# Latent attention: output products from seven half-block products, and half of the divisions moved to ScalarE

## Chip, core and metric

The kernel runs on one core of one Trainium2 chip. The metric is the device time of one execution in microseconds (us); the time before is 2025.44 us, the median of three runs (2025.08, 2025.44, 2031.71).

## The reference, cut to what matters

The program is a stack of eight layers on x, two sequences of 512 tokens with 512 features each, all in float32. The change touches the third and the fifth layer. The fifth is latent attention with 32 heads:

```python
x = x + L0_attn_a(layernorm(x)); x = x + L0_ffn(layernorm(x))
x = x + L0_attn_b(layernorm(x)); x = x + L0_ffn(layernorm(x))   # attn_b: grouped queries
x = x + L1_attn_a(layernorm(x)); x = x + L1_ffn(layernorm(x))   # attn_a: latent attention
...
def L1_attn_a(x, wq_a, q_norm_w, wq_b, wkv_a, kv_norm_w, wkv_b, wo):
    q = rms_norm(x @ wq_a.T, q_norm_w) @ wq_b.T          # 32 heads, 128 + 64 features
    kv_c, k_pe = split(x @ wkv_a.T)                      # 64 latents, 64 rotary features
    k_nope, v = split(rms_norm(kv_c, kv_norm_w) @ wkv_b.T)
    scores = (q_nope . k_nope + rope(q_pe) . rope(k_pe)) * scale, causal
    out = softmax(scores) @ v                            # (b, s, 32 * 128)
    return out @ wo.T                                    # wo.T: (4096, 512)
```

## The kernel before

`attn_mla` keeps the values as 64 latents per token. For every group of eight heads (`grp`, four of them) `fold_values` multiplies the value weights into the output weights, head by head, into one tile `fold` of 512 x 512 (four chunks of 128 partitions, two heads of 64 latents in each). The context of eight heads is then a tile `ctxT` of 512 latents x 512 tokens, and the output of the group is the product of the two, added to x.

The work goes over eight pairs `m` of a head group and a sequence (`grp`, `b`), with `b` changing fastest, and over eight heads `h` in each: 64 units. The first eight units are in `opening`; the other 56 are in the loop at L1594. Per unit the loop issues:

- on every even head, `queries` for the heads two further on (TensorE, 3 us) and `rotate`: two instructions on VectorE (L1461, L1462), and three on GpSimd (L1465 and twice L1468);
- `exponents`: four rows of score products (L274), and for each row one masked minimum on VectorE (L285) and one exponential on ScalarE (L295);
- `normalise`: a reciprocal on VectorE (L303), and the division of the four rows (128, 256, 384 and 512 wide) by four GpSimd instructions (L310);
- `turned_head`: two block transposes of the head before on VectorE (L322, L323).

Beside the heads of pair `m` the function `beside` finishes the pair before it. At `h` = 1 `values` runs the value products (L350) and copies the four banks to `ctxT` (L364, L365). At `h` = 3, 4, 6 and 7 `output` makes the product for one tile of 128 tokens by a chain of four matmuls of 128x128 by 512 (L183), and adds it to x on VectorE (L250). Where `b` is 1, `fold_values` runs at `h` = 0 and `fold_keys` at `h` = 4 and 5. After the last unit, `m` = 8 has the values and outputs of the last pair alone, with the layer norms of the first sequence for the next layer beside them.

TensorE and VectorE run in the order in which the code is written here (`manual_schedule`); ScalarE's and GpSimd's instructions in the loop are put in order by the framework's scheduler, by priority and readiness. All of PSUM is one tile `held` of eight banks, which `turn` hands out in a ring; `reserve` takes one bank out of the ring.

The third layer, `attn_gqa`, already makes its output products (L1163) as seven products of half blocks for all but its last pair: `out_sums` (L1115) and `context_sums` (L1130) form the sums of blocks on GpSimd (L1127, L1137 to L1140), `out_product` (L1145) makes a product and adds it to the rows with `add_quarter` (L247). Its divisions are all on ScalarE (L308).

Of the kernel before, what the change touches and what calls it, by code (L numbers as in the profile page):

```python
# [31 lines left out]
F32 = mybir.dt.float32  # L32
# [3 lines left out]
ALU = mybir.AluOpType  # L36
# [10 lines left out]
class Block:  # L47
# [251 lines left out]

    def normalise(self, probs, total, scalar=False):  # L300

        inv = self.sm(NT, "invs")
        self.nc.vector.reciprocal(inv, total)  # L303
        for qt in range(NT):
            row = probs[:, self.ROW[qt] : self.ROW[qt] + self.KEYS[qt][1] - self.KEYS[qt][0]]
            each = inv[:, qt : qt + 1]
            if scalar:
                self.nc.scalar.activation(row, row, AF.Identity, scale=each)  # L308
            else:
                self.nc.gpsimd.tensor_scalar(row, row, each, 1.0, ALU.mult, ALU.mult)  # L310
# [604 lines left out]


def attn_gqa(k, a, bound, block):

# [9 lines left out]
    with ExitStack() as ctx:  # L928
# [162 lines left out]
        def softmax(m, j):  # L1091
            probs = k.other().rearrange("p t s -> p (t s)")
            k.normalise(probs, k.exponents(qs.pop((m, j)), keys[m], probs), scalar=True)
            return probs
# [13 lines left out]

        left, right = slice(0, D // 2), slice(D // 2, D)
        sums = [lp.tile([P, 2, S // 2], F32, tag="c_sum", name="c_sum", bufs=3) for i in range(3)]  # L1110
        room = [k.w.tile([P, 3, D // 2], F32, tag="w3", name="wo_sum", bufs=6) for i in range(2)]
        held = [(0, 0), (0, 1), (0, 2), (1, 0), (1, 1), (1, 2)]
        outs = {}

        def out_sums(m, part):  # L1115

            wo = w[m]["wo"]
            b11, b12, b21, b22 = (  # L1120
                [wo[:, 2 * r + i, c] for i in range(2)] for r in range(2) for c in (left, right)
            )
            t1, t2, t4 = ([room[n][:, o] for n, o in held[2 * i : 2 * i + 2]] for i in range(3))
            steps = (t1, b12, b11), (t2, b22, t1), (b12, b22, b12), (t4, b21, t2)
            for out, x, y in steps[2 * part : 2 * part + 2]:
                for i in range(2):
                    nc.gpsimd.tensor_tensor(out[i], x[i], y[i], ALU.subtract)  # L1127
            outs[m] = b11, b21, b22, t1, t2, b12, t4

        def context_sums(m):  # L1130
            c = ctxs[m]
            a11, a12, a21, a22 = (
                c[:, 2 * r : 2 * r + 2, t] for t in (first, second) for r in range(2)
            )
            s1, s2, s4 = sums
            op = nc.gpsimd.tensor_tensor
            op(s1, a21, a22, ALU.add)  # L1137
            op(a21, a11, a21, ALU.subtract)
            op(s2, s1, a11, ALU.subtract)
            op(s4, a12, s2, ALU.subtract)  # L1140
            ctxs[m] = a11, a12, a22, s1, s2, a21, s4

        begun = {}

        def out_product(m, n):  # L1145


            a11, a12, a22, s1, s2, s3, s4 = ctxs[m]
            b11, b21, b22, t1, t2, t3, t4 = outs[m]
            lhsT, rhs = {  # L1150
                1: (a11, b11), 2: (a12, b21), 3: (s4, b22), 4: (a22, t4),
                5: (s1, t1), 6: (s2, t2), 7: (s3, t3),
            }[n]
            after = n in (5, 6)
            if n == 1:
                begun[m] = k.reserve()
            ps = begun[m] if n in (1, 5, 6) else k.turn()
            if n == 5:
                k.reserved = None
            for t in range(2):  # L1160
                out = ps[:, bass.ts(t, D // 2)]
                for i in range(2):
                    nc.tensor.matmul(  # L1163
                        out, lhsT[:, i, bass.ts(t, P)], rhs[i],
                        start=not (after or t or i), stop=i == 1, skip_group_check=True,
                    )
            at = groups[m][1] * NT
            for rows, columns in {
                1: ((0, left),), 2: ((0, left),), 3: ((0, right),), 4: ((2, left),),
                5: ((0, right), (2, right)), 6: ((2, left),), 7: ((2, left), (2, right)),  # L1170
            }[n]:
                k.add_quarter(at + rows, columns, ps)

# [12 lines left out]
        def beside(m, j):  # L1186
# [9 lines left out]
            if before is not None and j == 1:  # L1196
                values(before)
                if m < len(groups):
                    spread_values(m)
                if summed:  # L1200
                    context_sums(before)
            if m == G - 1 and j < 2:
# [18 lines left out]
            if summed and 0 < j < 3:  # L1221
                out_sums(before, j - 1)
            if before is not None and not summed and j > 1:
# [54 lines left out]
def attn_mla(k, a):  # L1278
# [9 lines left out]
    with ExitStack() as ctx:  # L1288
# [7 lines left out]
        def load(g):  # L1296
            w = dict(
                qn=k.load(a["m_wqn"][g], [P, J, QL], "w3", 6),
                wk=k.load(a["m_wk"][g], [P, J, KL], "w3", 6),
                wv=k.load(a["m_wv"][g], [P, J, KL], "w3", 6),  # L1300
                wo=k.load(a["m_wo"][g], [P, J, D], "w8", 5),
                lat=lp.tile([P, J, KL], F32, tag="q_lat", name="q_lat", bufs=3),
                pe=lp.tile([P, J, 64], F32, tag="q_pe", name="q_pe", bufs=3),
                rest=lp.tile([P, J, 64], F32, tag="q_rest", name="q_rest", bufs=3),
            )
            nc.sync.dma_start(out=w["pe"], in_=a["m_wpe0"][g])
            nc.sync.dma_start(out=w["rest"][64:128], in_=a["m_wpe1"][g])
# [283 lines left out]
        with tc.manual_schedule(engines=engines | {mybir.EngineType.Activation, mybir.EngineType.Pool}):  # L1591
            opening()
        with tc.manual_schedule(engines=engines):
            for n in range(E, len(units) + E):  # L1594
# [514 lines left out]
def _layout(i):  # L2109
# [60 lines left out]
    wkvb = i["L1_attn_a_wkv_b"].reshape(8, 4, 256, 64)  # L2170
    o["m_wk"] = wkvb[:, :, :128].transpose(0, 2, 1, 3)
    o["m_wv"] = wkvb[:, :, 128:].transpose(0, 2, 1, 3)
    o["m_wo"] = i["L1_attn_a_wo"].T.reshape(8, 4, P, D).transpose(0, 2, 1, 3)
# [38 lines left out]
```

## Time and profile before

| What | Value |
| --- | --- |
| median of three runs | 2025.44 us |
| the profiled execution: time, span from first to last instruction | 2033.69 us, 2031.7 us |
| TensorE matmul (PE) busy | 1950.3 us, 96% |
| VectorE (DVE), ScalarE (ACT), GpSimd (POOL) busy | 68%, 43%, 51% |
| granted TensorE clock, mean over the span | 0.985 |
| `attn_gqa`, most of it (300 to 1110 us): PE busy | 801 of 810 us |
| `attn_mla`, the loop (1208 to 1598 us): PE busy | 374.47 of 390 us |
| in the loop: DVE, ACT, POOL busy | 254.12, 185.02, 222.74 us |

Times of single instructions are in ns, stretches and sums in us from the start of the span. A float32 matmul shows as two records, so that a chain of four matmuls is eight records. A record's duration is longer than the step from one record to the next, since matmuls are pipelined; what a product occupies on TensorE is read from start to start.

### The profile page before, as it was taken

Reading aid. Unit: us, or ns where it says so; the run is one execution under the profiler, and the core shown is the slowest. Engines: PE = TensorE matmul, PEld = TensorE weight load, DVE = VectorE, ACT = ScalarE, POOL = GpSimd, SP = SyncE. Lnnn points to the kernel's source line nnn. Section 1 sums busy time; section 2 is a strip of 40 time slices with the busy share of each in tenths; the row PEclk is TensorE's granted clock in tenths of the full one; section 3 lists DMA queues with packets and bytes.
Section 4 is the critical chain, followed back from the end, with each engine's and each line's share of the span. In section 5 each row is a group of like instructions: output and inputs, shape, how many; then the busy total and the mean of one; then the engine's idle time right before and its main releaser. Section 6 shows DMA issues by size and latency. Waiting matters only on the chain. (4 is left out here: it accounts for less than half of the span.)

```text
span 2031.7 us, 40110 instructions
## 1 busy us (share of the span) xinstructions
PE 1950.3 (96%) x15424; PEld 1171.7 (58%) x15424; DVE 1390.0 (68%) x3585; ACT 882.8 (43%) x2350; POOL 1036.5 (51%) x1212
## 2 busy tenths in 40 slices
PE   9889989999999999999999999999999899997999
PEld 5333346777777777777775544454544545654554
DVE  8778748767776677767775577666566675845854
ACT  3676723444444444444442365444545211631451
POOL 4411146687755678777752175555465634224221
PEclk9988999999999999999999999999999999998999
DMA  4010212122221223222222220020201003002001
GB/s 137 11 42 1 73 63 73 53 84 98 101 73 44 83 78 103 100 81 74 73 75 90 76 83 26 5 73 1 73 1 43 6 6 47 2 2 41 2 2 42
DMA packets 69789, 108.92 MB, mean 54 GB/s; under 512 B 13522, under 2 KB 50386, under 8 KB 62548
## 3 DMA queue, kind: packets, MB, share of 16 engines
q1 hardware_dynamic: 68660, 103.10, 16.2%
q8 instruction: 125, 2.05, 0.4%
q10 hardware_dynamic: 640, 1.05, 0.3%
q0 software_dynamic: 288, 2.10, 0.3%
q14 instruction: 76, 0.62, 0.1%
HBM read 80.00 MB, written 4.19 MB: 41 GB/s over the span
## 5 line engine op out<-in xcount | busy, mean ns | idle before, releaser
L295 ACT ACTIVATE room<-room,nmax 128x128 f32<-128x128 f32 (+3 forms) x384 | 212.9, 558 | 354.4 <-DVE nmax L285 351.5
L274 PE MATMUL held<-kT,q 128*32 128x64 f32 (+15 forms) x4096 | 264.1, 396 | 20.0 <-DVE invs L303 12.5
L285 DVE CUSTOM_DVE_ANT_0 room<-held,mask 128x128 f32<-128x128 f32 (+3 forms) x384 | 179.0, 487 | 82.7 <-PE held L274 76.9
L274 PEld LDWEIGHTS held<-kT,q 128*32 128x32 f32 x4096 | 141.5, 110 | 111.8 <-issue 30.3
L350 PE MATMUL held<-turned,vals 32*128 32x384 f32 (+7 forms) x2784 | 187.8, 416 | 1.3 <-issue 1.3
L587 DVE TENSOR_REDUCE nm<-held 128x1 f32<-128x512 f32 x256 | 161.8, 682 | 36.9 <-PE held L617 31.0
L350 PEld LDWEIGHTS held<-turned,vals 32*128 32x128 f32 (+1 forms) x2784 | 149.5, 167 | 37.8 <-issue 23.0
L308 ACT ACTIVATE room<-room,invs 128x128 f32<-128x128 f32 (+3 forms) x256 | 122.8, 550 | 31.3 <-DVE invs L303 31.2
L323 DVE STREAM_TRANSPOSE turned<-room 128x1152 f32<-128x1152 f32 x80 | 108.2, 1365 | 35.1 <-ACT room L308 21.6
L236 POOL TENSOR_TENSOR rstd<-ve,mhalf 128x1 f32<-128x1 f32 x64 | 37.8, 594 | 174.7 <-DVE ve L234 170.4
L183 PE MATMUL held<-fold,ctxT 128*128 128x512 f32 x256 | 117.8, 604 | 0.6 <-ACT ctxT L364 0.6
L247 DVE TENSOR_TENSOR rows<-rows,held 128x512 f32<-128x512 f32 x135 | 89.4, 681 | 36.3 <-PE held L1163 35.8
L1070 POOL TENSOR_TENSOR q<-q,room 128x256 f32<-128x256 f32 x64 | 45.4, 731 | 127.5 <-DVE q L1053 124.0
L295 ACT ACTIVATE probs<-probs,nmax 128x128 f32<-128x128 f32 (+3 forms) x128 | 71.1, 556 | 66.5 <-DVE nmax L285 65.3
L310 POOL TENSOR_SCALAR probs<-probs,invs 128x128 f32<-128x128 f32 (+3 forms) x128 | 66.0, 536 | 59.6 <-DVE invs L303 57.5
L1088 POOL TENSOR_TENSOR q<-q,cosq 128x512 f32<-128x512 f32 x60 | 85.9, 1432 | 20.5 <-DVE t L1085 20.5
L1044 PE MATMUL held<-room,w 128*128 128x256 f32 x384 | 95.1, 384 | 0.0
L183 PE MATMUL sc<-w,room 128*128 128x512 f32 x208 | 92.7, 592 | 0.0
L579 PEld LDWEIGHTS held<-keys,qs 32*128 32x128 f32 x256 | 31.1, 189 | 101.4 <-DVE nm L587 71.2
L1089 POOL TENSOR_TENSOR q<-q,t 128x512 f32<-128x512 f32 x64 | 86.3, 1348 | 5.6 <-DVE q L1088 1.9
L1465 POOL TENSOR_TENSOR t<-t,sinq 128x512 f32<-128x512 f32 x31 | 39.6, 1279 | 95.9 <-DVE invs L303 95.9
L1163 PE MATMUL held<-w,ctxT 128*128 128x256 f32 x360 | 86.5, 383 | 0.5 <-ACT ctxT L364 0.5
(349 smaller groups left out, 4982.3 us busy)
## 6 DMA issues: line engine op xcount, KB each, us to landing
w<-in_b_wq SPq DMA_DIRECT2D x16, 1024.0 KB, 4.8
w<-in_b_wo SPq DMA_DIRECT2D x16, 1024.0 KB, 5.0
vals<-v SPq DMA_DIRECT2D x256, 64.0 KB, 2.0
w<-in_m_wo SPq DMA_DIRECT2D x8, 1024.0 KB, 5.3
w<-in_b_wk SPq DMA_DIRECT2D x16, 256.0 KB, 2.7
w<-in_b_wupv SPq DMA_DIRECT2D x16, 256.0 KB, 2.6
w<-in_m_wqn SPq DMA_DIRECT2D x8, 384.0 KB, 3.0
rows<-in_x SPq DMA_DIRECT2D x8, 256.0 KB, 4.7
```

The lines of the kernel that those rows point to most:

```text
L183: last = self.nc.tensor.matmul(out, lhsT, rhs, start=(i == 0), stop=(i == len(pairs) - 1))
L247: self.nc.vector.tensor_tensor(x, x, ps.rearrange("p (t d) -> p t d", t=2), op)
L274: nc.tensor.matmul(ps[32 * i : 32 * i + 32, a - lo : b - lo], q[:, at : at + 32], keys[:, a:b], start=True, stop=True,)
L285: nc.vector.tensor_tensor_reduce(out=row, in0=ps[:, :kv], in1=self.mask_back[:, :kv] if qt % 2 else self.mask[:, S - kv :], op0=ALU.add, o ...
L295: nc.scalar.activation(row, row, AF.Exp, bias=nmax, scale=-1.0, accum_out=total[:, qt : qt + 1])
L308: self.nc.scalar.activation(row, row, AF.Identity, scale=each)
L323: self.nc.vector.transpose(out[:, :last], probs[:, :last])
L350: self.nc.tensor.matmul(out[:, :, :n], values(i, j), rhs, start=(j == blocks[0]), stop=(j == stop[i]),)
L587: k.latest = nc.vector.tensor_reduce(nm[u % 2][:, qt, at : at + 1], ps, AX.X, ALU.max, negate=True).ins
L1044: nc.tensor.matmul(out, lhsT[:, c], rhs[:, c], start=c == 0, stop=c == 1)
L1089: nc.gpsimd.tensor_tensor(q, q, t2, ALU.add)
L1163: nc.tensor.matmul(out, lhsT[:, i, bass.ts(t, P)], rhs[i], start=not (after or t or i), stop=i == 1, skip_group_check=True,)
```

## The change

In `attn_mla` the output of a pair is no longer four chains but seven products of half blocks. The context C (tokens x latents) and the folded weights M (latents x features) are cut into 2 x 2 blocks of 256 x 256. Each product is two tiles of 128 tokens by two chunks of 128 latents: four matmuls of 128x128 by 256. The sums of blocks that they need are formed on GpSimd: per pair four of the context (`context_sums`, in two parts at `h` = 2 and 3), per head group six instructions for the weights (`weight_sums`, in two parts at `h` = 1 and 2 of the pair with `b` = 1; one block of `fold` is overwritten). `STEPS` puts products 1 and 2 at `h` = 3, 6 and 4 at `h` = 4, 5 and 3 at `h` = 6, and 7 at `h` = 7; `TAIL` is the order for the last pair. Product 1's bank is reserved; 6 and 5 are accumulated on top of it, so that it is read three times and comes back to the ring after product 5. The seven products are added to x by nine additions of 128 x (2 x 256).

In the loop of `attn_mla` the rows of 128 and of 512 are divided on ScalarE, those of 256 and 384 on GpSimd as before; `opening` is unchanged in this. The key and value weights of four heads come in by one DMA in place of two. `attn_gqa` uses the same class now; there two of its sums of weight blocks are one instruction of 512 each in place of two of 256, and the second and third context sum change places.

```diff
-    def normalise(self, probs, total, scalar=False):
+    def normalise(self, probs, total, scalar=()):
...
-            if scalar:
+            if qt in scalar:
                 self.nc.scalar.activation(row, row, AF.Identity, scale=each)
             else:
                 self.nc.gpsimd.tensor_scalar(row, row, each, 1.0, ALU.mult, ALU.mult)
...
+class HalfBlocks:
+    LEFT, RIGHT = slice(0, D // 2), slice(D // 2, D)
+    ADDED = {
+        1: ((0, LEFT),), 2: ((0, LEFT),), 3: ((0, RIGHT),), 4: ((2, LEFT),),
+        5: ((0, RIGHT), (2, RIGHT)), 6: ((2, LEFT),), 7: ((2, LEFT), (2, RIGHT)),
+    }
...
+    def weight_sums(self, key, wo, part):
+        a, b = self.held
+        op = lambda out, x, y: self.k.nc.gpsimd.tensor_tensor(out, x, y, ALU.subtract)
...
+        t1, t4 = a[:, 0:2], b[:, 1:3]
+        t2 = a[:, 2], b[:, 0]
+        if part == 0:
+            op(t1, b12, b11)
+            for i in range(2):
+                op(t2[i], b22[:, i], t1[:, i])
+        else:
+            op(b12, b22, b12)
+            for i in range(2):
+                op(t4[:, i], b21[:, i], t2[i])
...
+    def context_sums(self, c, part=None):
...
+        if part != 1:
+            op(s1, a21, a22, ALU.add)
+            op(s2, s1, a11, ALU.subtract)
+        if part != 0:
+            op(a21, a11, a21, ALU.subtract)
+            op(s4, a12, s2, ALU.subtract)
+        self.context = {1: a11, 2: a12, 3: s4, 4: a22, 5: s1, 6: s2, 7: a21}
+
+    def product(self, key, n, at):
+        k = self.k
+        lhsT, rhs = self.context[n], self.of[key][n]
+        after = n in (5, 6)
+        if n == 1:
+            self.begun = k.reserve()
+        ps = self.begun if n == 1 or after else k.turn()
+        if n == 5:
+            k.reserved = None
+        for t in range(2):
+            out = ps[:, bass.ts(t, D // 2)]
+            for i in range(2):
+                k.nc.tensor.matmul(
+                    out, lhsT[:, i, bass.ts(t, P)], rhs[i],
+                    start=not (after or t or i), stop=i == 1, skip_group_check=True,
+                )
+        for rows, columns in self.ADDED[n]:
+            k.add_quarter(at + rows, columns, ps)
...
-                wk=k.load(a["m_wk"][g], [P, J, KL], "w3", 6),
-                wv=k.load(a["m_wv"][g], [P, J, KL], "w3", 6),
+                wkv=k.load(a["m_wkv"][g], [P, 2, J, KL], "w3", 6),
...
-        def output(grp, b, t):
-            ps = k.turn()
-            c = ctxs[grp, b]
-            k.chain(ps, [(c[:, i, bass.ts(t, P)], ms[grp][:, i]) for i in range(J)])
-            k.add_to_x(b * NT + t, ps)
+        def begin_sums():
+            room = k.w.tile([P, 3, 2, S // 2], F32, tag="w8", name="c_sums", bufs=5)
+            return HalfBlocks(k, [room[:, i] for i in range(3)])
...
+        STEPS = {3: (1, 2), 4: (6, 4), 6: (5, 3), 7: (7,)}
+        TAIL = {3: (1, 2), 4: (4, 6), 6: (3, 5), 7: (7,)}
...
+            if before and h in (1, 2) and before[1] == 0:
+                halves.weight_sums(before[0], ms[before[0]], h - 1)
+            if before and h in (2, 3):
+                halves.context_sums(ctxs[before], h - 2)
             if before and h in (3, 4, 6, 7):
-                output(*before, (3, 4, 6, 7).index(h))
+                for n in (TAIL if last else STEPS)[h]:
+                    halves.product(before[0], n, before[1] * NT)
...
                 if n < len(units):
-                    k.normalise(probs[n % 2], total)
+                    k.normalise(probs[n % 2], total, (0, NT - 1))
```

More of the change, by code (lines that the diff above doesn't have):

```diff
@@ L914, in ffn_lora, with __init__ @@
                 k.layernorm(t, k.turn, back=True)
+class HalfBlocks:
+    LEFT, RIGHT = slice(0, D // 2), slice(D // 2, D)
+    ADDED = {
+        1: ((0, LEFT),),
+        2: ((0, LEFT),),
+        3: ((0, RIGHT),),
+        4: ((2, LEFT),),
+        5: ((0, RIGHT), (2, RIGHT)),
+        6: ((2, LEFT),),
+        7: ((2, LEFT), (2, RIGHT)),
+    }
+    def __init__(self, k, sums):
+        self.k, self.sums, self.of = k, sums, {}
+        self.held = [
+            k.w.tile([P, 3, D // 2], F32, tag="w3", name="wo_sum", bufs=6) for i in range(2)
+        ]
+    def weight_sums(self, key, wo, part):
+        a, b = self.held
+        op = lambda out, x, y: self.k.nc.gpsimd.tensor_tensor(out, x, y, ALU.subtract)
+        b11, b12, b21, b22 = (
+            wo[:, 2 * r : 2 * r + 2, c] for r in range(2) for c in (self.LEFT, self.RIGHT)
+        )
[9 more added lines that the diff above has]
+                op(t4[:, i], b21[:, i], t2[i])
+        pair = lambda x: (x[:, 0], x[:, 1])
+        self.of[key] = {
+            1: pair(b11), 2: pair(b21), 3: pair(b22), 4: pair(t4), 5: pair(t1), 6: t2, 7: pair(b12)
+        }
+    def context_sums(self, c, part=None):
+        first, second = slice(0, S // 2), slice(S // 2, S)
+        a11, a12, a21, a22 = (c[:, 2 * r : 2 * r + 2, t] for t in (first, second) for r in range(2))
+        s1, s2, s4 = self.sums
+        op = self.k.nc.gpsimd.tensor_tensor
+        if part != 1:
[20 more added lines that the diff above has]
+                    start=not (after or t or i), stop=i == 1, skip_group_check=True,
+                )
+        for rows, columns in self.ADDED[n]:
+            k.add_quarter(at + rows, columns, ps)
@@ L1092, in softmax @@
             probs = k.other().rearrange("p t s -> p (t s)")
-            k.normalise(probs, k.exponents(qs.pop((m, j)), keys[m], probs), scalar=True)
+            k.normalise(probs, k.exponents(qs.pop((m, j)), keys[m], probs), range(NT))
             return probs
@@ L1107, in output @@
             k.add_to_x(groups[m][1] * NT + t, ps)
-        left, right = slice(0, D // 2), slice(D // 2, D)
         sums = [lp.tile([P, 2, S // 2], F32, tag="c_sum", name="c_sum", bufs=3) for i in range(3)]
[L1111 to L1143, printed above, removed]
@@ L1145, in out_product @@
-        def out_product(m, n):
[L1148 to L1172, printed above, removed]
+        halves = HalfBlocks(k, sums)
@@ L1174, in attn_gqa @@
+        def out_product(m, n):
+            halves.product(m, n, groups[m][1] * NT)
         units = [(m, j) for m in range(len(groups)) for j in range(J)]
@@ L1200, in beside @@
                 if summed:
-                    context_sums(before)
+                    halves.context_sums(ctxs[before])
             if m == G - 1 and j < 2:
@@ L1221, in beside @@
             if summed and 0 < j < 3:
-                out_sums(before, j - 1)
+                halves.weight_sums(before, w[before]["wo"], j - 1)
             if before is not None and not summed and j > 1:
@@ L1305, in load @@
             )
+            w["wk"], w["wv"] = w["wkv"][:, 0], w["wkv"][:, 1]
             nc.sync.dma_start(out=w["pe"], in_=a["m_wpe0"][g])
@@ L1592, in attn_mla @@
             opening()
+        halves = begin_sums()
         with tc.manual_schedule(engines=engines):
@@ L2170, in _layout @@
     wkvb = i["L1_attn_a_wkv_b"].reshape(8, 4, 256, 64)
-    o["m_wk"] = wkvb[:, :, :128].transpose(0, 2, 1, 3)
-    o["m_wv"] = wkvb[:, :, 128:].transpose(0, 2, 1, 3)
+    o["m_wkv"] = wkvb.reshape(8, 4, 2, 128, 64).transpose(0, 3, 2, 1, 4)
     o["m_wo"] = i["L1_attn_a_wo"].T.reshape(8, 4, P, D).transpose(0, 2, 1, 3)
```

## The prediction

> **What bounds the kernel now.** I read the page, then the busy times of stretches, since a share over eight layers says nothing of one of them.
>
> ```profile
> core 0: us, PE busy (x) PEld busy (x) DVE busy (x) ACT busy (x) POOL busy (x), PEclk, DMA share, GB/s
> 300.00:1110.00 810.00, 801.01 (x6778) 592.28 (x6779) 578.54 (x1245) 344.11 (x957) 543.65 (x539) 1.00 0.25 78
> 1208.00:1598.00 390.00, 374.47 (x4203) 196.61 (x4191) 254.12 (x745) 185.02 (x567) 222.74 (x311) 1.00 0.10 34
> ```
>
> The first row is most of `attn_gqa`, the second the loop of `attn_mla`. In both TensorE is all but full, at the full granted clock. In the loop VectorE has 136 us free of 390, ScalarE 205, GpSimd 167. Next, what TensorE waits for there, in the view of waits:
>
> ```profile
> PE held L274 <- DVE invs L303: 11.1, 11, 1.1
> PE held L350 <- issue: 1.9, 2, 1.3
> PE held L350 <- DVE room L323: 1.3, 1, 1.3
> PE held L274 <- POOL q L1468: 1.2, 1, 1.2
> PE held L183 <- ACT ctxT L364: 0.6, 1, 0.6
> ```
>
> Eleven waits of about 1 us stand before the fourth score row of heads 1 and 3. VectorE is not overloaded there: ten banks have been handed out since the even head's rotary product, the ring has eight, and the row waits until the shuffle (L1462) has left that bank. GpSimd holds TensorE up once, for 1.2 us. So matmul time removed from this loop is time gained, unless another engine falls behind. The price of a product is read from start to start in the timeline; here heads 4 to 7 of one pair:
>
> ```profile
> 1291.63 3.70 PE L183 MATMUL held<-fold,ctxT 128*128 128x512 f32 x8
> 1295.26 2.04 PE L274 MATMUL held<-kT,q 128*32 128x32 f32 x32
> ...
> 1302.18 3.70 PE L183 MATMUL held<-fold,ctxT 128*128 128x512 f32 x8
> 1305.81 2.04 PE L274 MATMUL held<-kT,q 128*32 128x32 f32 x32
> 1307.78 3.70 PE L183 MATMUL held<-fold,ctxT 128*128 128x512 f32 x8
> 1311.32 1.02 PE L1444 MATMUL held<-lat,q_lat 128*128 128x512 f32 x2
> ```
>
> An output tile takes 3.63, 3.63 and 3.54 us; the pair's first (1283.25 to 1286.79) 3.54. The same half-block products as the new ones stand in `attn_gqa`:
>
> ```profile
> 483.96 1.99 PE L1163 MATMUL held<-wo_sum,c_sum 128*128 128x256 f32 x8
> 485.79 1.89 PE L1163 MATMUL held<-wo_sum,ctxT 128*128 128x256 f32 x8
> 487.52 3.73 PE L183 MATMUL held<-w,ckvT 128*128 128x128 f32 x32
> ```
>
> 1.83 and 1.73 us. The rows that price the rest:
>
> ```profile
> L310 POOL TENSOR_SCALAR probs<-probs,invs 128x512 f32<-128x512 f32 x29 | 20.2, 698 | 0.0
> L310 POOL TENSOR_SCALAR probs<-probs,invs 128x128 f32<-128x128 f32 x28 | 10.5, 374 | 59.2 <-DVE invs L303 57.5
> L308 ACT ACTIVATE room<-room,invs 128x512 f32<-128x512 f32 x64 | 45.2, 707 | 0.0
> L308 ACT ACTIVATE room<-room,invs 128x128 f32<-128x128 f32 x64 | 25.7, 402 | 31.3 <-DVE invs L303 31.2
> L1137 POOL TENSOR_TENSOR c_sum<-ctxT 128x512 f32<-128x512 f32 x15 | 19.2, 1279 | 15.3 <-ACT ctxT L365 15.3
> L1127 POOL TENSOR_TENSOR wo_sum<-w,wo_sum 128x256 f32<-128x256 f32 x60 | 49.9, 844 | 1.1
> L247 DVE TENSOR_TENSOR rows<-rows,held 128x512 f32<-128x512 f32 x135 | 89.4, 681 | 36.3 <-PE held L1163 35.8
> ```
>
> **1. Matmuls, on the path.** Before, a pair costs 2 x 3.63 + 2 x 3.54 = 14.34 us. After, seven products: at most 3 x 3.56 + 1.83 = 12.5, at least 7 x 1.73 = 12.1. That is 1.8 to 2.2 us a pair; I take 2.0, and 16.0 us for eight pairs. The Trainium skill speaks against it: Perfetto Trace Analysis, Matmuls, says that larger matmuls are more efficient than smaller ones. TensorE: Matmul & The Clock Gate gives about 2.5 ns that each back-to-back matmul costs beside its columns; the 192 records more would by that take an estimated 0.5 us of the gain. The rows show (1.83 + 1.73) / (3.63 + 3.54) = 0.497 for half the columns, so nothing is lost at this width.
>
> **2. VectorE.** Nine additions for four, 5 x 0.68 = 3.4 us a pair, beside 17 us that VectorE has free per pair. The place matters. From head 6's first score row to head 1, VectorE's own chain, by its rows in the timeline between 1248.2 and 1265.6, becomes: head 6's minima 2.27 and rotary 1.23, reciprocal 0.1, head 5's transposes 1.55, three additions 2.0, head 7's minima 2.1, head 6's transposes 1.55, reciprocal 0.1, two additions 1.3, head 0's minima 2.3, shuffle and product 1.2: 15.7 us, begun 0.5 behind TensorE. TensorE's own path to the same bank is 2.0 + 3.5 + 2.0 + 1.8 + 2.9 + 2.0 + 1.2 = 15.4, where it was 17.2 with a wait of 0.94 at its end (18.1). So the fourth row of head 1 can start after 16.2, and 1.9 of the 2.0 stay. With head 7's second score row now waiting for product 5's additions (the reserved bank comes round there) I charge 0.3 us on the four pairs without weight folding: 1.2 us. The other pairs have 4 us more TensorE work at head 0 to cover it. Bounds: 0, and 3.4 x 8 = 27 were nothing hidden.
>
> **3. GpSimd.** Removed: 0.37 + 0.70 = 1.07 us in each of 56 heads, 60 us. Added: context sums 4 x 1.28 x 8 = 41, weight sums (2 x 1.28 + 4 x 0.8) x 4 = 23. The total stays; the time of day changes. In the pairs with weight sums, heads 1 to 3 hold 11 us of sums beside their rotary and division work (1.07 a head and 3.9 at head 2). GpSimd stood idle before head 1's division for 5.88 us, during the value products, which takes in the first 2.9 us or more; then four context and three weight instructions must pass before products 6, 4, 3 and 7, from 14 us later on. Queued behind them are head 4's rotary sums, which TensorE's score products need: they end 1.3 us before they are wanted now, and the shorter division gives 1.07 more. Bounds: a gain of 1.2 us (the one wait on GpSimd gone), to 5.1 us in each of four pairs, 20.4, where all sums go first. I take 0.1 a pair, since GpSimd is light for the rest.
>
> **4. ScalarE.** 0.40 + 0.71 = 1.11 us a head, 62 us: 247 of 390 busy. It is queued between the exponentials of one head and the next, where ScalarE idles 2 to 5 us waiting for the next minima. Only at head 1 is it late: the reciprocal ends at 1277.55, and copies for the queries and head 2's exponentials, due at 1278.23, start at 1278.7: 0.4 us, into VectorE's 2.4 us free before head 4. Bounds 0 to 0.4 us in every head, 25.6; I take 0.1 a pair. Steps 3 and 4 together: 1.6 us.
>
> **5. The end.** The rows of the second sequence were finished one by one, and the norms of the first three lay beside the remaining outputs: 0.69 + 0.18 + 0.15 + 0.55 = 1.6 us each on VectorE. Now they are finished by products 5 and 7, so up to 4.7 us of norms move into the next layer's start, where TensorE waits for the router's VectorE chain (2.46, 0.99, 0.95 and 1.37 us between 1622 and 1641). Against this, the last addition has to go before the next layer's banks are free, two additions now: 0.7. Bounds 0 to 5.4; I take 1.2, since the norms are wanted four tiles later.
>
> **6. Edits at nothing.** `attn_gqa` saves GpSimd 15 x (0.18 + 0.22) = 6 us, under a TensorE that is 99% busy. One weight DMA less per load; the loads are used a head or more later. If either cover failed, I allow 1 us each way.
>
> **The sum.** -16.0 + 1.2 + 1.6 + 1.2 = -12.0 us. On the profiled execution 2033.7 - 12.0 = 2021.7; that execution lies 8.2 us above the median of the runs, so 2025.4 - 12.0 = 2013.4 us, or 0.6% less. About 0.5%, 10.1 us, is what a measurement of this kernel can tell from no change.
>
> **The rivals.** (a) The gain is given back by GpSimd's queue: sums ahead of head 2's rotary and head 4's, TensorE waiting at the score products. For it: 11 us of sums in three heads, an order not written by hand. Against it: 167 us free, one wait of 1.2 us today. Each microsecond of wait per pair takes 8 us; between 0.3 and 2.5 us a pair the result is 2015 to 2033, mostly within 0.5%. The same band holds if VectorE's chain of step 2 is late.
>
> (b) Slower: ScalarE's queue. A division waits for the reciprocal, which stands on VectorE behind the transposes of the head before (odd heads) or the rotary (even heads); the next head's exponentials wait behind the division, and the next reciprocal behind those. If this closes on itself it costs each of 56 heads; from 0.4 us a head (22 us, which with -12 makes +10) it decides, and at the full 1.11 us it is 62 us. At 0.45: 25 - 12 = +13, 2038 us. Against it: 2 to 5 us idle before the exponentials today.
>
> (c) More than forecast: 2.2 us a pair and none of the charges of steps 2 to 5: -17.6, 2007.8.
>
> **How the numbers follow.** The forecast with its own range of 2008 to 2015.3: 0.56; (c) 0.04; (a) 0.28; (b) 0.12. Faster by over 0.5%: 0.60; within: 0.28; slower: 0.12. The range 2008 to 2027 leaves out (b), (c) and the upper end of (a), about 0.2.
>
> **What would show it.** Right: half-block products at 1.73 to 1.83 us from start to start in the loop; the step from one pair's value products to the next pair's shorter by 1.5 to 2 us; PE busy as full as now; half of the L310 records gone in the loop, ScalarE near 245 us there; waits of TensorE still on the shuffle's bank. Wrong: new waits of the score products on GpSimd's rotary sums (a), ScalarE without idle time before its exponentials (b), gaps before the transposes on VectorE, or over 3 us more between the last product and the router's first transpose.

## The result and the profile after

The changed kernel takes 2033.38 us (median of 22 runs, 2028.59 to 2041.31), the kernel before 2030.29 us in the 22 runs beside it: a ratio of the means of 1.0027, with a 95% interval of 1.0015 to 1.004. That is slower by about 5.5 us, within the 0.5% bound that the prediction set for "the same", and not the 12 us faster that it forecast.

The first 290 us, whose layers are the same in all kernels here, differ between executions by stretches in which the granted clock is half (20.5 us at 183 us in the profiled execution of before, 3.4 in that of e2 below), so I compare the latent attention alone, by the starts of TensorE's steps in the timeline: from the first value products (L350 at `m` = 1) to the last (`m` = 8), and from there to the next layer's router, at its first transpose (from `hw`).

| us | first to last value products | last value products themselves | from their end to the router | sum |
| --- | --- | --- | --- | --- |
| before | 376.05 | 10.14 | 25.45 | 411.64 |
| after | 371.93 | 13.00 | 33.15 | 418.08 |

The loop is 4.1 us shorter, where the sum had 14 of products less 2.8 of waits; the end is 10.6 us longer, where it had 1.2 of charges less 2 for the eighth pair's products. The busy times of the two stretches (busy us and number of instructions of PE, PEld, DVE, ACT and POOL; granted clock, DMA share, GB/s):

```profile
core 0: us, PE busy (x) PEld busy (x) DVE busy (x) ACT busy (x) POOL busy (x), PEclk, DMA share, GB/s
300.00:1110.00 810.00, 801.85 (x6784) 592.68 (x6781) 578.33 (x1246) 344.45 (x957) 537.99 (x510) 1.00 0.25 79
1208.00:1598.00 390.00, 368.50 (x4376) 230.30 (x4368) 272.83 (x783) 238.07 (x682) 220.17 (x250) 0.99 0.12 40
```

`attn_gqa` has not moved. In the loop ScalarE took over 53 us, VectorE 19, and GpSimd kept its total; no engine is near full but TensorE, which now idles more than before: 21.5 us of 390, where it was 15.5. What it waited for from 1195 to 1650 us, the view of waits (total, times, longest):

```profile
PE held L274 <- DVE invs L303: 11.2, 11, 1.1
PE held L221 <- DVE xn L208: 4.0, 1, 4.0
PE held L350 <- issue: 3.9, 3, 1.7
PE held L274 <- DVE rows L247: 3.1, 3, 1.0
PE held L350 <- DVE room L323: 2.8, 1, 2.8
...
PE pj L183 <- DVE ln_mv L200: 1.6, 1, 1.6
PE held L274 <- POOL q L1490: 1.4, 2, 1.2
```

The first row is unchanged (11.1 before): the eleven waits for the shuffle's bank stay. Rows two, four and six are new, the third and the fifth have doubled. Each belongs to one step of the work. In the timeline, heads 4, 6 and 7 of the pair `m` = 2:

```profile
1291.62 1.99 PE L990 MATMUL held<-wo_sum,c_sums 128*128 128x256 f32 x8
1293.45 1.89 PE L990 MATMUL held<-wo_sum,ctxT 128*128 128x256 f32 x8
1295.27 2.04 PE L274 MATMUL held<-kT,q 128*32 128x32 f32 x32
...
1304.01 1.89 PE L990 MATMUL held<-fold,c_sums 128*128 128x256 f32 x8
1305.83 0.70 PE L274 MATMUL held<-kT,q 128*32 128x32 f32 x16
1307.56 1.55 PE L274 MATMUL held<-kT,q 128*32 128x288 f32 x16 [1.03 <-DVE rows L247]
1309.05 1.99 PE L990 MATMUL held<-fold,ctxT 128*128 128x256 f32 x8
1310.88 1.02 PE L1466 MATMUL held<-lat,q_lat 128*128 128x512 f32 x2
```

A half-block product takes 1.83 us from start to start, two together 3.65. The single product 7 takes 1.83, where a whole tile took 3.54: that is the whole gain of a pair. In front of it head 7's scores stop for 1.03 us at their third row, until the two additions of product 5 (L247, ended at 1307.51) have freed product 1's bank: their step is 3.21 us, and 1.97 where nothing waits.

The end, GpSimd's queue and TensorE beside it, first before the change:

```profile
1601.74 0.55 POOL L236 TENSOR_TENSOR rstd<-ve,mhalf 128x1 f32<-128x1 f32 x1
1602.45 1.14 PE L221 MATMUL held<-ident,xn 128*128 128x128 f32 x8
```

and after:

```profile
1601.44 1.45 POOL L971 TENSOR_TENSOR ctxT<-ctxT 128x512 f32<-128x512 f32 x1
1602.86 1.26 POOL L972 TENSOR_TENSOR c_sums<-ctxT,c_sums 128x512 f32<-128x512 f32 x1
1604.08 1.26 POOL L241 TENSOR_TENSOR rows<-rows,bias 128x512 f32<-128x512 f32 x1
1605.29 0.55 POOL L236 TENSOR_TENSOR rstd<-ve,mhalf 128x1 f32<-128x1 f32 x1
```

```profile
1601.82 0.66 PE L221 MATMUL held<-ident,xn 128*128 128x128 f32 x4
1606.48 0.66 PE L221 MATMUL held<-ident,xn 128*128 128x128 f32 x4 [4.00 <-DVE xn L208]
```

The fourth norm's reciprocal root (0.55 us) was ready to run at 1602.8 and stood behind two context sums and a bias addition until 1605.29; TensorE waited 4 us for it with five of the last pair's seven products queued behind. And the last value products, before and after:

```profile
1587.13 1.09 PE L350 MATMUL held<-turned,vals 32*64 32x512 f32 x8
1589.50 0.66 PE L350 MATMUL held<-room,vals 32*64 32x512 f32 x4 [1.29 <-DVE room L323]
```

```profile
1583.53 1.09 PE L350 MATMUL held<-turned,vals 32*64 32x512 f32 x8
1587.37 1.13 PE L350 MATMUL held<-room,vals 32*64 32x512 f32 x4 [2.75 <-DVE room L323]
```

In the trace's time they start 3.6 us earlier, and they wait 1.5 us longer for the transposed probabilities of the last head. Finally the stretch around a "wait for issue", one of those in the value products beside the weight loads, after the change:

```profile
1327.00:1331.00 4.00, 2.33 (x85) 1.78 (x76) 0.00 (x0) 0.00 (x0) 1.39 (x3) 0.98 0.31 119
1331.00:1335.00 4.00, 4.00 (x35) 1.93 (x25) 2.29 (x5) 2.07 (x8) 1.01 (x1) 0.60 0.00 0
```

TensorE idles 1.67 of the first 4 us, and the granted clock of the next 4 is 0.60: half clock from 1330.8 to 1334.2. The queries there take 4.01 us in place of 2.97. Before the change there was no half clock between 289.6 and 1719.8 us; now there are 17 us of it between 1330 and 1638, each piece in or behind a wait of TensorE.

So the 6.4 us lost between the first value products and the router are: products -11.6 (seven pairs at -1.65), the bank at head 7 +3.7 (three pairs), value products of the loop +3.6, queries at half clock +1.0, a wait on GpSimd that is gone at 1575.9 us -1.0; together -4.2, and -4.1 is measured; then +2.9 in the last value products and +7.7 behind them, of which 4.2 at the transposes at 1606.48 and 3.5 in the products and the router's first steps behind them, at late norms and half clock.

### The profile page after: what moved, and what is told of

Read it like the earlier page. It is cut to its first block, busy times and chain, and to the rows that moved or that the text cites. A ratio compares the mean times of both kernels' runs of the same rounds, so it can differ in the third digit from the quotient of the medians.

```text
span 2039.1 us, 40553 instructions
## 1 busy us (share of the span) xinstructions
PE 1947.0 (95%) x15616; PEld 1212.5 (59%) x15616; DVE 1408.8 (69%) x3625; ACT 935.7 (46%) x2462; POOL 1035.2 (51%) x1126
## 3 DMA queue, kind: packets, MB, share of 16 engines
q1 hardware_dynamic: 67508, 103.10, 16.2%
## 5 line engine op out<-in xcount | busy, mean ns | idle before, releaser
L274 PE MATMUL held<-kT,q 128*32 128x64 f32 (+15 forms) x4096 | 264.7, 396 | 22.8 <-DVE invs L303 12.5
L350 PE MATMUL held<-turned,vals 32*128 32x384 f32 (+7 forms) x2784 | 189.9, 419 | 0.0
L587 DVE TENSOR_REDUCE nm<-held 128x1 f32<-128x512 f32 x256 | 161.9, 683 | 36.9 <-PE held L617 29.9
L350 PEld LDWEIGHTS held<-turned,vals 32*128 32x128 f32 (+1 forms) x2784 | 150.1, 168 | 36.2 <-issue 21.5
L308 ACT ACTIVATE room<-room,invs 128x128 f32<-128x128 f32 (+3 forms) x312 | 151.3, 551 | 42.3 <-DVE invs L303 42.2
L247 DVE TENSOR_TENSOR rows<-rows,held 128x512 f32<-128x512 f32 x207 | 135.8, 677 | 44.4 <-PE held L990 42.3
L183 PE MATMUL sc<-w,room 128*128 128x512 f32 x224 | 101.2, 599 | 0.0
L1169 POOL TENSOR_TENSOR q<-q,cosq 128x512 f32<-128x512 f32 x60 | 85.9, 1432 | 22.4 <-DVE t L1166 22.4
L620 ACT ACTIVATE pt<-held 128x512 f32<-128x512 f32 x128 | 69.6, 597 | 33.0 <-PE held L617 30.2
L579 PE MATMUL held<-keys,qs 32*128 32x512 f32 x256 | 78.6, 518 | 6.1 <-DVE nm L587 5.8
```

Source lines behind the costliest of these rows:

```text
L183: last = self.nc.tensor.matmul(out, lhsT, rhs, start=(i == 0), stop=(i == len(pairs) - 1))
L247: self.nc.vector.tensor_tensor(x, x, ps.rearrange("p (t d) -> p t d", t=2), op)
L274: nc.tensor.matmul(ps[32 * i : 32 * i + 32, a - lo : b - lo], q[:, at : at + 32], keys[:, a:b], start=True, stop=True,)
L350: self.nc.tensor.matmul(out[:, :, :n], values(i, j), rhs, start=(j == blocks[0]), stop=(j == stop[i]),)
L579: nc.tensor.matmul(ps, qs[b][rows[g], 4 * half + i, bass.ts(qt, P)], keys[b][rows[g]], start=True, stop=True,)
L587: k.latest = nc.vector.tensor_reduce(nm[u % 2][:, qt, at : at + 1], ps, AX.X, ALU.max, negate=True).ins
```

## The experiments

Theory A: the gain of the products is real, and it is lost in single places that have nothing to do with each other: a bank, weight loads, the queue of GpSimd at the end, the last head's chain. The rivals were those of the prediction: GpSimd's queue everywhere (a), ScalarE's queue (b). The columns of the table above, for the profiled execution of each, with the ratio to before:

| run | first to last | last value products | to the router | sum | ratio, 95% interval |
| --- | --- | --- | --- | --- | --- |
| e1_tail | 368.44 | 11.62 | 28.04 | 408.10 | 0.9999 [0.9985, 1.0014] |
| e2_bank | 368.77 | 11.62 | 33.96 | 414.35 | 1.0031 [1.0016, 1.0046] |
| e3_no_loads | 365.41 | 11.62 | 33.95 | 410.98 | 1.0012 [0.9994, 1.003] |
| e4_seven | 369.42 | 13.20 | 34.26 | 416.88 | 1.0041 [1.002, 1.0061] |
| e5_act_only | 374.16 | 10.10 | 25.43 | 409.69 | 0.999 [0.9976, 1.0004] |
| e6_pool_only | 367.23 | 13.55 | 33.77 | 414.55 | 1.0027 [1.0012, 1.0042] |
| e7_last_rows | 369.87 | 13.39 | 25.45 | 408.71 | 0.9979 [0.9964, 0.9995] |
| e8_early_all | 368.28 | 13.38 | 25.46 | 407.12 | 0.9982 [0.9969, 0.9995] |
| e9_three_groups | 366.83 | 10.10 | 25.43 | 402.36 | 0.996 [0.9946, 0.9975] |
| e10_three_early | 369.88 | 10.10 | 25.43 | 405.41 | 0.9984 [0.997, 0.9997] |

**e1_tail.** GpSimd in written order behind the last unit; `unit` is the loop's body, unchanged.

```diff
         with tc.manual_schedule(engines=engines):
-            for n in range(E, len(units) + E):
...
+            for n in range(E, len(units)):
+                unit(n)
+        with tc.manual_schedule(engines=engines | {mybir.EngineType.Pool}):
+            for n in range(len(units), len(units) + E):
+                unit(n)
```

> The changed kernel, with GpSimd in written order after the last head, so that both reciprocal roots of the next layer's norms stand before the four context sums. Theory A (the loss at the end is GpSimd's queue: the last root waited behind three sums and a bias addition, and TensorE 4.0 us for it): the 4.0 us wait before the transposes of row 3 falls under 0.7 us, the half-clock stretch after it goes, the last product starts 5 us earlier against the first, and the time is 4 to 6 us below the changed kernel, level with the kernel before within 0.2%. Theory B (the loss is the additions and norms on VectorE, which all four rows now need at once): the wait goes, but the first router transpose (hw) comes at most 2 us earlier.

The roots now run before the sums, and TensorE's wait is 0.78 us (timeline of GpSimd, then of TensorE):

```profile
1595.12 1.27 POOL L241 TENSOR_TENSOR rows<-rows,bias 128x512 f32<-128x512 f32 x1 [0.66 <-DVE xn L208]
1596.35 0.55 POOL L236 TENSOR_TENSOR rstd<-ve,mhalf 128x1 f32<-128x1 f32 x1
1596.86 1.27 POOL L968 TENSOR_TENSOR c_sums<-ctxT 128x512 f32<-128x512 f32 x1
```

```profile
1598.47 0.66 PE L221 MATMUL held<-ident,xn 128*128 128x128 f32 x4 [0.78 <-DVE xn L208]
```

The transposes' step falls from 5.15 to 1.87 us, the half clock behind it is gone, and 28.04 us are left to the router in place of 33.15. The ratio is back at 1. Of the 10.0 us that the sum fell, 5.1 are this order; the rest is 1.4 less half clock in the last value products and 3.5 in the loop, where the value products beside loads were cheaper in this execution (below).

**e2_bank.** Product 1's bank goes back to the ring at product 7 instead of 5; in `attn_gqa` it stays at 5.

```diff
-        if n == 5:
+        if n == self.last:
             k.reserved = None
...
-            return HalfBlocks(k, [room[:, i] for i in range(3)])
+            return HalfBlocks(k, [room[:, i] for i in range(3)], 7)
```

> The changed kernel, with product 1's bank kept out of the ring until product 7 instead of product 5, in the latent attention. Theory A (the third score row of head 7 waits for the additions of product 5, because the reserved bank comes round there): the three steps of 3.21 us for head 7's scores go back to 1.97 us, 3.7 us less in the loop, at most 1 us of it lost again at head 1. Theory B (VectorE as a whole is late in heads 6 and 7, the bank only shows it): the wait moves to another row or to the queries, the loop is within 1 us of the changed kernel's.

The three steps of 3.21 us are gone, all are 1.97. From the value products of `m` = 2 to those of `m` = 3 it is 53.31 us (after 54.54, before 54.94), and the loop is 3.2 us shorter. In the time of the whole kernel (1.0031) this can't be seen; the profiled execution of this run has its own half clock at 1436.0, at a query step of 4.62.

**e3_no_loads.** The third to eighth load leave out the big weights: the first groups' tiles are used in their place, so that the output is that of other weights.

```diff
+            first = w[g % 2] if g > 1 else dict(qn=..., wkv=..., wo=...)
```

> The changed kernel without the loads of the later head groups' large weights (the first group's three weight tiles are used for all four groups; the small rotary ones are still loaded). Theory A (in the value products TensorE runs out of instructions, whose own fetches stand behind 3 to 4 MB of weights started just before): the steps of the value products, 9.49, 8.31, 10.83, 8.31, 9.56, 8.31 and 8.46 us, are all 8.2 to 8.5, and the half-clock stretch at the third goes with its 1.0 us at the queries: 4 to 5 us less in the loop. Theory B (they wait for the transposes on VectorE): the long steps stay.

```profile
PE held L274 <- DVE rows L247: 3.1, 3, 1.0
...
PE held L350 <- issue: 0.3, 1, 0.3
```

The waits "for issue" fall from 3.9 us to 0.3 while the bank's stay; the value products beside the former loads take 8.40, 7.85 and 7.85 us, where they took 9.49, 10.83 and 9.56 (8.40, 8.84 and 9.47 before the change), and there is no half clock in the loop. It is 6.5 us shorter than after the change. With the bank's 3.7 taken off it would be 361.7: 14.4 below before. That compares with a kernel that pays for its loads too: the sum of those three steps was 26.7 us before and is 24.1 without loads, so 2.6 of the 14.4 are not the products', and the 11.8 left agree with seven pairs at 1.65. The gain of the products exists in the loop, and these two places took most of it. How much the loads cost varies: the three steps take 29.9 us after the change, between 27.1 and 29.6 in the six other half-block runs that load at the same heads, and 26.7 and 26.0 in the two kernels with whole tiles (before, e5). So the change makes it worse by 0.4 to 3.2 us against before, differently in each execution.

**e4_seven.** Product 7 of the last full pair is written at the next pair's head 0, so that its two additions stand behind the last head's transposes on VectorE.

```diff
-                for n in (TAIL if last else STEPS)[h]:
+                for n in (TAIL if last else STEPS)[h] if (m, h) != (len(groups) - 1, 7) else ():
                     halves.product(before[0], n, before[1] * NT)
+            if last and h == 0:
+                held = groups[m - 2]
+                halves.product(held[0], 7, held[1] * NT)
```

> The changed kernel, with product 7 of the pair before the last written behind the transposes of the last head: TensorE's order stays, its two additions follow the transposes on VectorE. Theory A (the last value products wait for a chain that does not shorten with the products: minima, exponentials, division, transposes, and now two additions in it): the last step of the value products falls from 13.0 us by 1.2 to 1.5 us and the half-clock stretch in it may go with another 1 us. Theory B (the chain waits for the division): no change, the transposes start when they do now.

Theory A is out, theory B holds: the last value products still take 13.20 us. The timeline says why:

```profile
1574.86 0.31 DVE L322 STREAM_TRANSPOSE room<-probs 128x128 f32<-128x128 f32 x1 [0.47 <-ACT probs L308]
1575.56 1.38 DVE L323 STREAM_TRANSPOSE room<-probs 128x1152 f32<-128x1152 f32 x1 [0.39 <-POOL probs L310]
...
1576.99 0.66 PE L350 MATMUL held<-room,vals 32*64 32x512 f32 x4 [2.64 <-DVE room L323]
```

With the additions out of the way VectorE waits for the divisions, and TensorE's wait is 2.64 in place of 2.75. From the start of the last head's scores to the end of its transposes it is 7.6 us here, 7.7 after and 7.9 before the change: a chain of scores, exponentials, reciprocal, divisions and transposes. The product in front of the value products covered 3.6 us of it before and covers 1.9 now. The 1.7 us saved at that place are not to be had while this chain stands.

**e5_act_only.** The kernel before, with the rows of 128 and 512 divided on ScalarE in its loop.

```diff
-                    k.normalise(probs[n % 2], total)
+                    k.normalise(probs[n % 2], total, (0, NT - 1))
```

> The kernel before with one part of the change alone: in the loop of latent attention the rows of 128 and 512 columns are divided on ScalarE, the other two on GpSimd; the output products stay four whole-row tiles. Theory A (the gain of the products is lost in waits at single places: bank, weight loads, the queue of GpSimd at the end; the divisions take no part): 0 us, time ratio 0.999 to 1.001, the stretch from the first value products to the last 376 us as before, steps of the value products within 0.3 us of before. Rival (b) of the prediction (the queue of ScalarE): 0.2 to 0.45 us more for each of 56 heads, 11 to 25 us in that stretch, ratio 1.005 to 1.012. A gain is possible too, at most the 1.2 us of the one wait on GpSimd.

The interval of the ratio holds 1. The loop is 1.9 us shorter, of which 1.0 is the wait on GpSimd before the last pair's score products (L1468: 1.2 us before, now 0.2) and most of the rest the value products beside loads. Rival (b) is out: nothing here costs each head.

**e6_pool_only.** The changed kernel with all divisions on GpSimd.

```diff
-                    k.normalise(probs[n % 2], total, (0, NT - 1))
+                    k.normalise(probs[n % 2], total)
```

> The changed kernel with all four divisions of a head back on GpSimd: the half-block products alone. Theory A: the same losses as in the changed kernel plus GpSimd falling behind, since 60 us of divisions come back on top of 64 us of sums: new waits of the score products on the rotary sums of GpSimd at heads 2 to 4 of pairs with weight sums, 1 to 3 us in each of four pairs; first value products to last 373 to 384 us (372 in the changed kernel), ratio to before 1.003 to 1.009. Rival (b) (ScalarE's queue is what takes the gain): the stretch falls by 5 us or more below 372, ratio 0.998 or less. Rival (a) as the prediction had it (GpSimd's queue is what matters everywhere): more than 384 us.

```profile
PE held L274 <- POOL q L1490: 2.4, 2, 1.2
...
PE held L274 <- DVE rows L247: 1.5, 3, 0.5
```

My expectation for theory A missed: GpSimd does not fall behind with 60 us more; it holds TensorE up twice for 1.2 us, and the loop takes 367.23 us, less than in the changed kernel. The bank's wait is halved (the score step is 2.67 us, not 3.21): in the changed kernel VectorE's reciprocal ahead of it, at 1304.70, waits 0.42 us for ScalarE's exponentials, and here it does not wait. The ratio is the changed kernel's, 1.0027: the ScalarE half of the change neither saves nor costs anything that these runs can tell. Rival (a) is out as a cost of each pair.

**e7_last_rows.** The changed kernel, its last pair by four whole tiles. `fold`'s overwritten block is restored first by a subtraction, and the context sums of this pair fall away.

```diff
-                for n in (TAIL if last else STEPS)[h]:
+                for n in () if last else STEPS[h]:
                     halves.product(before[0], n, before[1] * NT)
+                if last:
+                    output(*before, (3, 4, 6, 7).index(h))
```

> The changed kernel with the last pair's output products as four whole-row tiles, as before the change; one subtraction of GpSimd gives the folded weights back beforehand, and the context sums of the last pair fall away. Theory A (the end lost 10.6 us between the last value products and the router's first transpose, because the last reciprocal root stood behind two context sums and all norms came late): that stretch returns from 46.2 to 35.6 to 38 us (up to 1.5 more, as the last value products start with a longer wait), at the price of 1.7 us of product time; ratio to before 0.996 to 0.999. Rival (the end is long because the half blocks give the rows late, whatever the queue): cannot be told apart here, but together with the run that only put GpSimd in written order (39.7 us): if this run gives 35.6, the 4 us left there are the price of the half blocks in the last pair; if it gives 39 or more, they come from the last head's chain and not from the products.

From the end of the last value products to the router it is 25.45 us, exactly as before the change. With e1 this splits the 7.7 us: 5.1 were GpSimd's order, 2.6 the half blocks themselves, which finish the rows late. The value products still start behind 1.92 us of product 7, wait, and fall to half clock at 1583.8 (13.39). So from their start to the router it is 38.84 us, above the 35.6 to 38 expected, and the excess is the last head's chain. The ratio is below 1.

**e8_early_all.** e7 and e2 together, and the folding of the weights with the loads that it frees one head earlier.

```diff
-            if b == 1 and h == 0 and grp:
+            if b == 0 and h == 7 and grp:
                 fold_values(grp, range(J))
-            if more and h in (1, 2):
-                ws.setdefault(grp + 1, []).append(load(2 * grp + 1 + h))
+            if (b == 0 and h == 7 and 0 < grp < G // 2 - 1) or (m, h) == (1, 0):
+                ws[grp + 1] = [load(2 * grp + 2 + i) for i in range(2)]
```

> Three edits together: the weight folding of a group and the loads that it releases come one head earlier (head 7 of the pair before, instead of heads 0 to 2), the reserved bank is given back at product 7 instead of product 5, and the last pair's products are four whole-row tiles as in the run of the last rows. Theory A: value products at 8.3 to 8.6 us in the pairs with loads (9.5 to 10.8 in the changed kernel), no score step of 3.21 us, first value products to last 363 to 367 us (372 changed, 376 before), to the router's first transpose 36 to 38 us more; together 11 to 13 us below before, ratio 0.994 to 0.996. Rival (the transfers collide with the value products wherever they stand, since 3 MB take longer than one head): value products still at 9 or more in two of the three pairs, first to last 368 to 370, ratio 0.997 to 0.999.

The value products in those pairs take 8.31 us but for the first pair (10.13, with a wait of 1.28 us for the transposes), and no wait "for issue" is left there. Yet the loop is 368.28 us, not 363 to 367: without the folding between head 0 and head 1 three more score steps wait for the shuffle's bank and are 1.26 us longer each. That cover had been named in the prediction's step 2, and I took it away. The last value products keep their 13.38 us, and the ratio is 0.9982 where 0.994 to 0.996 were expected. Loop and ratio lie in the rival's ranges, but not by its mechanism.

**e9_three_groups.** Half blocks in the first three groups alone, and e2's bank; the last group's two pairs by whole tiles.

```diff
+            by_rows = before and before[0] == G // 2 - 1
...
-                for n in (TAIL if last else STEPS)[h]:
+                for n in () if by_rows else STEPS[h]:
                     halves.product(before[0], n, before[1] * NT)
+                if by_rows:
+                    output(*before, (3, 4, 6, 7).index(h))
```

> Half blocks in the first three groups (six pairs) alone, the last group's two pairs by whole-row tiles, so that the product before the last value products takes 3.6 us again and no half-block product stands after the loop; the reserved bank given back at product 7; weight folding and loads as in the changed kernel. Theory A (the 1.7 us that the half blocks save at the last pair's head 7 are no gain, since the last value products wait for the chain of scores, exponentials, divisions and transposes of the last head, 7.6 us long from the start of the scores, and the wait brings a stretch at half clock): the last value products at 10.1 to 10.4 us as before the change, no half clock near them, from their start to the router's first transpose 35.6; from the first value products to the last 369 to 373 (six pairs' gain of 1.7, less the collisions with loads); in all 405 to 408.5 from the first value products to the router, 411.6 before; ratio 0.997 to 0.9985. Rival (the chain of the last head is longer in itself because ScalarE takes part in its divisions): last value products at 11.6 or more, from their start to the router 37 or more.

2019.03 us beside 2026.13, faster than both kernels (0.996 of before; the changed one is at 1.0027). The loop is shorter than expected (366.83 us, not 369 to 373), and so the ratio is better. The end is that of before to 0.1 us, since the whole tile of 3.6 us again covers the last head's chain, with no half clock from 1184 to 1709 us, although ScalarE still divides there. That removes the rival of this run. The waits of TensorE:

```profile
PE held L274 <- DVE invs L303: 11.2, 11, 1.1
...
PE held L350 <- issue: 2.4, 4, 1.1
PE held L274 <- POOL q L1490: 1.4, 2, 1.2
PE held L350 <- DVE room L323: 1.2, 1, 1.2
```

**e10_three_early.** The same with e8's early folding and loads.

> The same with the weight folding and the loads that it releases one head earlier, as in the run of the three edits. Theory A: value products at 8.3 us beside the later loads (9.5 to 10 in the first pair), one more wait of 1.26 us for VectorE at head 1 in the three pairs that lose the folding as cover, last value products 10.1 to 10.4, to the router 35.6; in all 404 to 407 us from the first value products to the router, ratio 0.9965 to 0.998. Rival (the earlier loads give nothing, the waits only change their place): the same as the run of three groups within 1 us.

```profile
PE held L274 <- DVE invs L303: 14.3, 14, 1.1
...
PE held L350 <- DVE room L323: 2.5, 2, 1.2
```

No wait "for issue" is left, three waits for the shuffle's bank are added, and the sum is 3.05 us above e9's. It lies in theory A's range, but e9 had come out below its own, so that neither holds against e9: the earlier loads exchange one wait for another, and in these two executions at a loss.

## Why the prediction was wrong, step by step

The sum was -12.0 us; from the first value products to the router +6.4 were measured. The 18.4 between them, by the steps:

- **Step 1, matmuls: the term was mis-sized.** The half-block products cost what the rows of `attn_gqa` said, 0.5 of a whole one. What the Trainium skill (Perfetto Trace Analysis, Matmuls) says, that larger matmuls are more efficient, does not show at this width. But 3.56 + 2 x 3.65 + 1.83 = 12.69 us lies above the prediction's own upper bound of 12.5, as a pair of products beside a score step takes 3.65 like the whole tile it replaces: 1.65 us a pair and not 2.0. And the eighth pair has nothing to give: with whole tiles there the way to the router is 2.6 us shorter than with half blocks and GpSimd in written order (e7, e1). -11.6 in place of -16.0: 4.4 us.
- **Step 2, VectorE: the right place, the wrong size.** The chain was right: from head 6's scores to the fourth row of head 1 it is 16.4 us (1249.35 to 1265.76) where 16.2 were forecast, and the waits for the shuffle's bank are 11.2 us in all, 11.1 before. The wait of head 7's scores for product 5's additions was named and priced at 0.3 us in four pairs; it is 1.24 us in three (e2 takes it away). 0.5 of each comes from ScalarE's divisions (e6), an effect across two steps that the prediction priced one by one. 2.5 us.
- **Steps 3 and 4, the queues in the loop: right.** 1.6 us were charged; GpSimd took one wait away, -1.0, and neither engine held up each head (e5, e6). Step 4's upper bound of 25.6 us counts 64 heads; 0.4 us in the loop's 56 makes 22.4, as in rival (b). The other place on GpSimd, a wait of 1.17 us at 1206.5 before the first value products, came when the scheduler pulled weight sums ahead of the rotary sums.
- **Step 5, the end: the step that failed.** 1.2 us charged, bounds 0 to 5.4, 10.6 measured. It looked at the norms' VectorE time and not at whose queue their roots stand in. Step 3 had counted the context sums of GpSimd pair by pair, and rival (a) said that their order is not written by hand; at the last pair the same sums meet the norms' roots (e1: 5.1 us). The half blocks' late rows cost 2.6 (e7), inside step 5's bounds, and 2.9 came from the last head's chain with the half clock behind it. 9.4 us.
- **Step 6, edits at nothing: failed.** It counted one DMA less and looked at when the weights are used, not at when their slots come free: two `wo_sum` tiles and `c_sums` take slots of the weights' rings, and the merged tile is held until `fold_values`. Loads stood just before these value products in the kernel before too, but more stand there now: 4.72 MB in place of 2.62 between 1200 and 1224 us, 2.79 in place of 2.41 between 1319 and 1336. The value products take 3.6 us more, 3.2 of them in the three beside loads, and the queries at half clock 1.0 in this execution, where 1 us either way was allowed (e3).
- **The rivals.** Scaled to the prediction's median the result is 2030.9 us, in the band of (a), but not by its mechanism: no microsecond is lost per pair on GpSimd, and the one place on GpSimd that counted lies outside the loop. (b) had no part.

Of what was to show it right, the products' steps, ScalarE's 238 us and the shuffle's waits came as written; TensorE did not stay as full, and the way from one pair's value products to the next was shorter by 1.5 us or more in two of seven. Of what was to show it wrong, the last came as written: 12.2 us from the end of the last product to the router's first transpose, 8.8 before.

What stays open: why TensorE's "waits for issue" stop it. The Trainium skill, Runtime: NRT & Kernel Launch, Instruction fetch mechanics, says that instructions are refilled in blocks of 16 KB by DMA and that the cost of crossing a block is mostly hidden. The trace has such a packet of 16 KB at 1327.35 us, at the end of loads that had kept the DMA engines 0.8 to 0.9 busy, and TensorE idle from 1327.99 to 1329.66; without loads the wait is gone (e3). The other traces agree: all 24 waits "for issue" in the value products of the twelve runs end 1.2 to 1.6 us after such a packet has landed. In the first value products it starts 6.5 us after them in the changed kernel, which waits, and 4.5 before the change and 4.1 in e3, which don't. So it is likely that TensorE waited for this packet; no run moved the packets alone.

## What to carry to other kernels

A saving on the bound engine is worth nothing where the next thing is a chain of another kind: price the last round of a loop by itself, and look at which queue each of its small links stands in, above all on an engine whose order a scheduler makes. A change that takes buffers from a ring moves the transfers that use the ring, and with them what runs beside those transfers; so ask of every tile added whose slot it is. And where an algorithm wins only in the steady part, use it there and leave the last rounds as they were (e9, with e2's bank: 0.996, where the whole change gave 1.0027).

## What the runs showed of the hardware

- Half clock can follow waits far shorter than the 3.4 us pieces it comes in: 3.4 us of it behind a wait of 1.67 us. But waits of 1.80 (e1) and 2.04 us (e4) in the value products beside loads brought none, and a wait of 2.6 to 3.0 us in the last value products brought it in the changed kernel, e4, e6, e7 and e8 (13.0 to 13.6 us) and not in e1, e2 and e3 (11.62), so the length alone does not decide. The Trainium skill, TensorE: Matmul & The Clock Gate, The HAM clock gate, speaks of free-running windows of 3.4 us and of a drop after at least one idle window; the pieces have that length, and the drop came here with less idle time than one.
- The many small matmuls of the value products (232 records in 8.31 us) stopped for 0.9 to 1.7 us beside bulk loads in the changed kernel (0.2 to 2.0 in all runs), with no engine in the profile that they waited for, until 1.2 to 1.6 us after a packet of 16 KB of instructions had landed; in e3, without the weight loads, one stop of 0.3 was left.
